# A two-layer graph network on one core: the output rows of layer 1 completed by accumulating DMAs

## The chip, the core and the metric

The kernel runs on one core of one Trainium2 chip. The time is device time in microseconds (us), and lower is better. The core has a matrix engine (TensorE, in the profile PE), an elementwise engine (VectorE, DVE), an activation engine (ScalarE, ACT), a general engine (GpSimd, POOL) and SyncE (SP), which here only issues DMAs. Each engine works through a queue of its own in order; they wait for each other by semaphores. SBUF is the on-chip memory; PSUM is the memory into which TensorE writes.

## What is computed

Two layers over N = 4096 nodes of 512 features, with a dense 4096 x 4096 matrix `adj`:

```python
h = relu(layernorm(x))
x = x + softmax(q @ k.T * scale + 2 * adj) @ v          # layer 0; q, k, v are projections of h
h = relu(layernorm(x))                                  # layer 1
nX = (h @ W) as 8 heads of 64, normalized per head, times a_ln, plus b_ln
kg = leaky_relu(at1 + at2.T) * adj                      # per head, at1 and at2 from nX
y = softmax(where(adj != 0, kg, -32768)) @ nX + nX      # "+ nX": the own features
x = x + elu(y)                                          # the residual
```

ELU is `y` where y is positive and `exp(y) - 1` elsewhere, so `elu(y) = relu(y) + (exp(-relu(-y)) - 1)`. The change is in how the last two lines are formed.

## The kernel before

The work has two stages. Layer 0 runs over 8 chunks of 512 target rows and 32 tiles of 128 source rows. It is led by TensorE. At the end of each chunk it writes the finished rows of layer 1's input to DRAM (`store_rows`, L457, into `x1_d`) and, spread over the next tiles, prepares layer 1: features, their statistics, and `own` (L358), which GpSimd computes and SyncE stores to `own_d`. `own` holds the own features with the constant that goes with them.

Layer 1 runs over 512 steps (`STEPS`, L897): 8 chunks of target rows, in each 2 groups of four heads (`hg`), in each 32 source tiles (`jt`). So a group of heads is 32 steps, and there are 16 groups. One step n does this:

- `z_sums` (L964), TensorE: the logits of four heads into two PSUM pairs `d`.
- `relu` (L987), ScalarE: relu of one pair into the SBUF tile `t`.
- `leaky` (L992), VectorE: for each of the other two heads a maximum and an addition (L999), then a multiplication by the adjacency tile `g` (L1004), of one head or, in a "light" step, of two; then the addition that ends the leaky relu of the first two heads (L1005).
- `weigh` (L1007), GpSimd: the multiplication by `g` of the remaining three heads, or of two in a light step (L1012). In the profile these are operations of 128x1536 and 128x1024.
- `exponent` (L1014), ScalarE, three steps later; `values` (L1017), TensorE, four steps later.

Which steps are light is a set of numbers (`light`, L904). The order is written by hand: every call under `seq` keeps its place in its engine's queue. DMAs without `seq` are placed by the scheduler.

When a group's last `values` is issued, `finish` (L1033) enters the group's remaining work into `later` under the following steps; `extra` then emits it at the middle or end of these. At step offsets 0 to 2 the sums are copied, turned into rows by TensorE and divided by their last column (`divide`, L1056), which also adds `own`. ELU follows with `minus`, `exps`, `positive` and `less_one` on ScalarE, `elu` (L1081) and `close` (L1085) on GpSimd, at offsets 4 to 10; `close` adds the residual `xi` and has SyncE store the result. `load_rows` (L956) loads `xi` and `own` for a group at its step 20: four DMAs of 256 KB, in pieces of 512 bytes.

Of the kernel before, what the change touches and what calls it, by code (L numbers as in the profile page):

```python
# [10 lines left out]
F32 = mybir.dt.float32  # L11
BF16 = mybir.dt.bfloat16
AF = mybir.ActivationFunctionType
ALU = mybir.AluOpType
# [4 lines left out]
P = 128  # L19
N = 4096  # L20
D = 512
NH = 8
HD = 64
NB = N // P
SB = 4
# [11 lines left out]
NI = N // GC  # L37
# [41 lines left out]
def fast_path(  # L79
# [18 lines left out]
    nc = tc.nc  # L98
    seq = tc.keep_in_program_order
# [14 lines left out]
    dram = ctx.enter_context(tc.tile_pool(name="dram", bufs=1, space=DRAM))  # L114
# [22 lines left out]
    s_d = dram.tile([NS, P, 4, KC // 2, 2, P], F32, name="s_d")  # L137
    q_d = dram.tile([NI, P, KC, GC], F32, name="q_d")
    t_d = dram.tile([NI, P, 4, KC // 2, GC // 2], F32, name="t_d")
    x1_d = dram.tile([N, D], F32, name="x1_d")  # L140

    gT_d = dram.tile([NB, P, N], F32, name="gT_d")
    nT_d = dram.tile([NB, P, N], BF16, name="nT_d")
# [4 lines left out]
    z1_d = dram.tile([P, 2, N], BF16, name="z1_d")  # L148

    nX_d = dram.tile([NB, P, D], F32, name="nX_d")  # L150

    own_d = dram.tile([N, D], F32, name="own_d")
    u4_d = dram.tile([NB, NH, P], F32, name="u4_d")
    at2_d = dram.tile([NB, P, NH], F32, name="at2_d")

    def inverse_root(engine, pool, v, n, name):

# [82 lines left out]
    def make_ready(ic, x1s, small, at_step, gap, last):  # L240

        n = SB * NH
# [3 lines left out]
        rows = slice(ic * SB, (ic + 1) * SB)  # L246
# [111 lines left out]
        def own(b):  # L358
            o = prep.tile([P, NH, HD], F32, name="own", tag="prod", bufs=2)
            seq(nc.gpsimd.tensor_mul(o, features(b), over_heads(aln_sb)))  # L360
            seq(nc.gpsimd.tensor_add(o, o, over_heads(bln2_sb)))
            nc.sync.dma_start(
                out=own_d[ts(ic * SB + b, P), :], in_=o.rearrange("p h e -> p (h e)")
            )

        def split():

# [59 lines left out]
        for b in range(SB):  # L427
            d = (0 if last else 2) + gap * b
# [27 lines left out]

    def store_rows(ic, x1s):  # L457
        for b in range(SB):
            seq(nc.sync.dma_start(out=x1_d[ts(ic * SB + b, P), :], in_=x1s[b]))


    with tc.tile_pool(name="early", bufs=2) as early, tc.tile_pool(name="kv", bufs=1) as kv:
        aa.extend(kv.tile([P, NH, HD], F32, name=f"a{e}_sb") for e in (1, 2))
        v = kv.tile([P, NB, D], F32, name="v")
# [68 lines left out]
        with tc.tile_pool(name="proj_c", bufs=1) as pc, tc.tile_pool(  # L533
            name="proj", bufs=2
# [137 lines left out]
            for sb in range(1, NS):  # L672
# [4 lines left out]
                if sb == 1:  # L677
                    seq(nc.sync.dma_start(
                        out=w1_sb.rearrange("p k h e -> p k (h e)"),
                        in_=w1.rearrange("(k p) o -> p k o", p=P),  # L680
# [16 lines left out]
        with tc.tile_pool(name="attn", bufs=2) as work, tc.tile_pool(  # L697
            name="attn_ps", bufs=2, space=PSUM
# [142 lines left out]
            for s in range(0, n_tiles, 2):  # L841
                ic, jt = TILES[s]
# [48 lines left out]
    with tc.tile_pool(name="ga_in", bufs=2) as inputs, tc.tile_pool(  # L891
# [8 lines left out]
        inverses = gat.tile([P, NI, 2, 2, 2, 4], F32, name="inverses")  # L900
        loads, logits, zs, groups = {}, {}, {}, {}


        light = {n for n in range(n_steps) if n % NB in (1, 8, 12, 13, 19, 25)}  # L904
        later = {}

        def load_adj(q):
# [40 lines left out]
        def pair_rows(ap, ic, hg):  # L948

            r, c = cols(ic, hg)  # L950
            return [
                ap[r, c.start + f * P : c.start + (f + 1) * P].rearrange("(b p) d -> p b d", p=P)
                for f in range(2)
            ]

        def load_rows(n):  # L956
            ic, hg, _ = STEPS[n]
            for name, src in (("xi", x1_d), ("own", own_d)):
                t = work.tile([P, 2, SB, 2 * HD], F32, name=name, tag=name, bufs=1)
                for f, ap in enumerate(pair_rows(src, ic, hg)):  # L960
                    nc.sync.dma_start(out=t[:, f], in_=ap)
                groups[ic, hg][name] = t

        def z_sums(n):  # L964

# [67 lines left out]
        def finish(n, ic, hg):  # L1033

            grp = groups.pop((ic, hg))
            ob = work.tile([P, 2, GC], F32, name="ob", tag="ob", bufs=1)
            y = grp["own"].rearrange("p f b (h e) -> p f (b h) e", e=HD)

            def room():
                grp["e"] = work.tile([P, 2, SB * 2, HD], F32, name="e", tag="ob", bufs=1)  # L1040

            def copies():
                for hf in range(2):
                    seq(nc.scalar.copy(ob[:, hf, :], grp["acc"][hf]))

            def to_rows(hf):
                pt = psum.tile([P, 2, GC], F32, name="pt1", tag="d", bufs=3)
                for b in range(SB):
                    col = (b % 2) * 2 * HB
                    seq(nc.tensor.matmul(  # L1050
                        pt[:, b // 2, col : col + 2 * HB], ob[:, hf, ts(b, P)],
                        back.rearrange("p e c -> p (e c)"), start=True, stop=True,
                    ))
                grp["pt"] = pt[:, :, 0 : 4 * HB].rearrange("p k (q c) -> p k q c", c=HB)

            def divide(hf):  # L1056
                v = grp.pop("pt")
                rinv = inverses[:, ic, hg, hf]
                seq(nc.vector.reciprocal(rinv, v[:, :, :, HD]))
                v = v[:, :, :, 0:HD]  # L1060
                seq(nc.vector.tensor_mul(v, v, rinv.unsqueeze(3).to_broadcast([P, 2, 4, HD])))
                own = y[:, hf].rearrange("p (k q) e -> p k q e", k=2)
                seq(nc.vector.tensor_add(own, v, own))

            def flat(t):
                return t.rearrange("p f q e -> p (f q e)")

            def minus(hf):
                seq(nc.scalar.activation(grp["e"][:, hf], y[:, hf], AF.Relu, scale=-1.0))

            def exps(hf):
                e = grp["e"][:, hf]
                seq(nc.scalar.activation(e, e, AF.Exp, scale=-1.0))

            def positive():
                seq(nc.scalar.activation(flat(y), flat(y), AF.Relu))

            def less_one():
                seq(nc.scalar.add(flat(grp["e"]), flat(grp["e"]), -1.0))

            def elu():  # L1081
                e = flat(grp["e"])
                seq(nc.gpsimd.tensor_add(e, e, flat(y)))  # L1083

            def close():  # L1085
                e = grp["e"]
                seq(nc.gpsimd.tensor_add(  # L1087
                    flat(e), flat(e), grp["xi"].rearrange("p f b d -> p (f b d)")
                ))
                for f, ap in enumerate(pair_rows(out, ic, hg)):  # L1090
                    nc.sync.dma_start(
                        out=ap, in_=e[:, f].rearrange("p (b h) e -> p b (h e)", h=2)
                    )

            for d, place, f in (
                (0, "mid", copies),
                (1, "mid", lambda: to_rows(0)), (1, "end", lambda: divide(0)),
                (2, "mid", lambda: to_rows(1)), (2, "end", lambda: divide(1)),
                (4, "end", room), (4, "end", lambda: minus(0)), (5, "end", lambda: minus(1)),
                (6, "end", lambda: exps(0)), (6, "end", positive), (7, "end", lambda: exps(1)),  # L1100
                (8, "end", less_one),
                (9, "end", elu), (10, "end", close),
            ):
                later.setdefault((n + d, place), []).append(f)

# [30 lines left out]
            for f in later.pop((n, place), []):  # L1136
                f()

        for n in range(n_steps + 15):

            q = n // JB + 1
            if n == 1:
# [1 line left out]
            if n % JB == (2 if q == NS - 1 else 0) and q < n_steps // JB:  # L1144
                load_adj(q)
                if q < NS:
                    load_features(q)
            if n < n_steps and STEPS[n][2] == 20:
                load_rows(n)
            if n + 10 < n_steps and STEPS[n + 10][2] == 0:  # L1150
                open_group(n + 10, nc.sync)
            extra(n, "top")
# [447 lines left out]
```

## Time and profile before

| what | value |
|---|---|
| median of 3 runs | 3955.43 us (3955.2 to 3957.88) |
| profiled execution | 3958.11 us |
| its span | 3956.2 us |
| TensorE busy | 3699.6 us, 94% |
| VectorE busy | 2915.4 us, 74% |
| GpSimd busy | 2501.9 us, 63% |
| ScalarE busy | 1779.3 us, 45% |
| mean TensorE clock granted | 0.99 |
| first VectorE operation of layer 1 (L999) | at 2092.05 us |

A share of the span is an average over two stages. In the page's row of 40 slices (a digit is the busy share in tenths) the two can be told apart:

```profile
PE   8989999999999999999997799999999999999997
...
DVE  5435556565565656556556799999999999999997
ACT  1001011111111111111114688888888888888887
POOL 3432225243342525234156899999999999999998
```

Layer 0 is the part in which only PE stands at 9. Layer 1 begins at about slice 22, and from there PE, VectorE and GpSimd are all at 9. In that second part the largest groups of instructions are, with count, busy time and mean duration of one, and then the idle time of the engine before them and what ended it (window from 2200 us to the end):

```profile
L1012 POOL TENSOR_TENSOR t<-t,g 128x1536 f32<-128x1536 f32 x401 | 1381.3, 3502 | 42.2 <-DVE t L1005 42.2
...
L1012 POOL TENSOR_TENSOR t<-t,g 128x1024 f32<-128x1024 f32 x92 | 220.7, 2399 | 18.6 <-DVE t L1005 13.5 <-DVE nX L1119 5.0
...
L1087 POOL TENSOR_TENSOR e<-e,xi 128x1024 f32<-128x1024 f32 x16 | 38.2, 2386 | 0.1
L1083 POOL TENSOR_TENSOR e<-e,own 128x1024 f32<-128x1024 f32 x16 | 38.0, 2376 | 12.3 <-ACT e L1079 12.3
...
L1061 DVE TENSOR_TENSOR pt<-pt,inverses 128x512 f32<-128x512 f32 x32 | 22.4, 700 | 1.1
L1063 DVE TENSOR_TENSOR own<-pt,own 128x512 f32<-128x512 f32 x32 | 22.1, 691 | 1.1
```

L1083 and L1087 are GpSimd's two additions at the end of a group, L1063 is VectorE's addition of `own`. The durations of neighbours overlap by some 0.05 us, so that sums of durations come out a little above the elapsed time.

### The profile page before, as it was taken

To read this page: it belongs to the slowest core of one execution; us is meant where nothing else is said; L and a number is where in the kernel's file an instruction comes from. 1 tells how busy PE (TensorE), PEld (TensorE's weight loads), DVE (VectorE), ACT (ScalarE), POOL (GpSimd) and SP (SyncE) were. 2 spreads that over 40 slices of the span, in tenths; PEclk is the share of its full clock that TensorE was granted. 3 is DMA by queue.
4 is the path that set the end of the run, shared out by engine and by line. 5 is a ranking of instruction groups with operands and counts; after the bars stand their busy time and mean duration, and the time that the engine had idled before them with its cause. 6 is when DMAs were issued, how large, how long until landed. Compare 5 with 4: busy or idle time off the path is not lost. (4 is left out here: it accounts for less than half of the span.)

```text
span 3956.2 us, 48595 instructions
## 1 busy us (share of the span) xinstructions
PE 3699.6 (94%) x17418; PEld 1720.8 (43%) x17418; DVE 2915.4 (74%) x4331; ACT 1779.3 (45%) x1581; POOL 2501.9 (63%) x1305
## 2 busy tenths in 40 slices
PE   8989999999999999999997799999999999999997
PEld 4446666666666666666662222222222222222222
DVE  5435556565565656556556799999999999999997
ACT  1001011111111111111114688888888888888887
POOL 3432225243342525234156899999999999999998
PEclk9999999999999999999998999999999999999999
DMA  6466666767675766758557766666666666665563
GB/s 205 178 201 193 204 183 199 206 187 218 177 228 158 217 192 183 222 174 230 151 174 190 191 186 187 184 186 175 169 180 181 184 181 184 180 185 172 172 181 111
DMA packets 624059, 737.79 MB, mean 186 GB/s; under 512 B 83904, under 2 KB 467136, under 8 KB 604352
## 3 DMA queue, kind: packets, MB, share of 16 engines
q1 hardware_dynamic: 621744, 732.83, 64.5%
q8 instruction: 138, 2.26, 0.2%
q10 hardware_dynamic: 2064, 1.77, 0.2%
q14 instruction: 113, 0.93, 0.1%
HBM read 562.23 MB, written 172.23 MB: 186 GB/s over the span
## 5 line engine op out<-in xcount | busy, mean ns | idle before, releaser
L1012 POOL TENSOR_TENSOR t<-t,g 128x1536 f32<-128x1536 f32 (+1 forms) x512 | 1655.3, 3293 | 98.3 <-DVE t L1005 66.4
L1028 PE MATMUL acc<-t,nX 128*64 128x512 f32 x4096 | 994.1, 606 | 41.0 <-ACT t L1015 35.9
L752 POOL TENSOR_TENSOR total<-total,aT 128x512 f32<-128x512 f32 x248 | 340.4, 1372 | 1060.1 <-ACT aT L747 1053.0
L1015 ACT ACTIVATE t<-t 128x2048 f32<-128x2048 f32 x512 | 974.9, 1904 | 2.0 <-POOL t L1012 2.0
L762 PE MATMUL acc<-v,aT 128*128 128x512 f32 x2048 | 961.7, 592 | 0.0
L747 ACT ACTIVATE aT<-aT 128x512 f32<-128x512 f32 x256 | 161.2, 630 | 1323.4 <-DVE aT L742 1315.4
L989 ACT ACTIVATE t<-d 128x1024 f32<-128x1024 f32 x512 | 524.8, 1025 | 319.4 <-PE d L981 319.2
L1005 DVE TENSOR_TENSOR t<-t,d 128x1024 f32<-128x1024 f32 x512 | 619.9, 1211 | 6.6 <-ACT t L989 6.6
L973 PE MATMUL d<-z,z 6*128 6x512 bf16 x2048 | 382.7, 387 | 140.5 <-DVE t L1004 76.5
L762 PEld LDWEIGHTS acc<-v,aT 128*128 128x128 f32 x2048 | 389.1, 190 | 273.1 <-issue 245.1
L1028 PEld LDWEIGHTS acc<-t,nX 128*64 128x64 f32 x4096 | 250.2, 136 | 552.1 <-issue 351.8
L999 DVE SCALAR_TENSOR_TENSOR d<-u,at2m,d 128x512 f32<-128x512 f32 x608 | 456.2, 750 | 33.3 <-PE d L981 29.8
L742 DVE TENSOR_TENSOR aT<-aT,X 128x256 f32<-128x256 f32 x512 | 214.8, 419 | 279.9 <-PE X L734 276.8
L1004 DVE TENSOR_TENSOR t<-d,g 128x512 f32<-128x512 f32 (+1 forms) x512 | 402.0, 785 | 16.6 <-DMA g<-gT_d 7.0
L973 PEld LDWEIGHTS <-z 6*128 6x128 bf16 x2048 | 94.4, 91 | 663.2 <-issue 400.9
L742 DVE TENSOR_TENSOR aT<-aT,Z 128x256 f32<-128x256 f32 x384 | 159.5, 415 | 291.3 <-PE Z L734 286.7
L999 DVE SCALAR_TENSOR_TENSOR t<-u,at2m,d 128x512 f32<-128x512 f32 x416 | 310.8, 747 | 43.2 <-DVE d L999 1.4
L981 PE MATMUL d<-nb,ident_b 64*64 64x512 bf16 x2048 | 319.9, 391 | 2.7 <-DMA nb<-nT_d 2.7
L981 PE MATMUL d<-nx,ident_b 64*64 64x512 bf16 x2048 | 320.3, 391 | 1.1 <-DMA nx<-nT_d 1.1
L726 DVE SCALAR_TENSOR_TENSOR gs<-ng,aT 128x512 f32<-128x512 bf16 x256 | 285.9, 1117 | 10.4 <-DMA gT_d<-gs 1.8
L734 PE MATMUL Z<-qt,hS 128*128 128x256 f32 x1024 | 265.9, 382 | 8.7 <-DVE aT L742 8.3
L734 PE MATMUL X<-qt,hS 128*128 128x256 f32 x1024 | 264.0, 380 | 0.0
(171 smaller groups left out, 3204.2 us busy)
## 6 DMA issues: line engine op xcount, KB each, us to landing
g<-gT_d SPq DMA_DIRECT2D x128, 1024.0 KB, 5.5
ag<-in_adj_dram SPq DMA_DIRECT2D x256, 256.0 KB, 5.7
hT<-h_d SPq DMA_DIRECT2D x64, 1024.0 KB, 5.9
hS<-s_d SPq DMA_DIRECT2D x64, 1024.0 KB, 8.2
gT_d<-gs SPq DMA_DIRECT2D x256, 256.0 KB, 3.0
nb<-nT_d SPq DMA_DIRECT2D x128, 512.0 KB, 4.5
nx<-nT_d SPq DMA_DIRECT2D x256, 256.0 KB, 5.4
nT_d<-ng SPq DMA_DIRECT2D x256, 128.0 KB, 3.4
```

Of the source, the lines that this page charges most:

```text
L734: seq(nc.tensor.matmul(out, a, b, start=start and k == 0, stop=k == 1, skip_group_check=not start,))
L742: seq(nc.vector.tensor_add(p, p, part))
L762: seq(nc.tensor.matmul(sums[ic][b], probs[s][:, ts(b, P)], v[:, jt, :], start=jt == 0, stop=jt == NB - 1))
L973: seq(nc.tensor.matmul(pair[hh // 2][:, hh % 2, :], z2[rows, ts(jt % JB, P)], groups[ic, hg]["z1"][rows, :], start=True, stop=False,))
L981: seq(nc.tensor.matmul(pair[hh // 2][ts(c, HD), hh % 2, :], ident_b[rows, rows], masks[r != c][rows, jt % JB, :], start=False, stop=True,))
L989: seq(nc.scalar.activation(t[:, 0:2, :], zs[n][0], AF.Relu, scale=4.0))
L999: seq(nc.vector.scalar_tensor_tensor(pair[1][:, e, :] if e > 1 - mine else t[:, 2, :], u4[:, e, :], at2m[:, jt, h : h + 1], pair[1][:, e, ...
L1004: seq(nc.vector.tensor_mul(t[:, HG - mine : HG, :], pair[1][:, 2 - mine : 2, :], g))
L1005: seq(nc.vector.tensor_add(t[:, 0:2, :], t[:, 0:2, :], pair[0]))
L1012: seq(nc.gpsimd.tensor_mul(t[:, 0:mine, :], t[:, 0:mine, :], g))
L1015: seq(nc.scalar.activation(logits[n], logits[n], AF.Exp))
L1028: seq(nc.tensor.matmul(grp["acc"][hf][ts(e, HD), :], nX[jt // SB][:, jt % SB, hg * HG + 2 * hf + e, :], t[:, 2 * hf + e, :], start=jt == 0 ...
```

## The change

Three elementwise additions of `finish` become accumulating DMAs, issued from GpSimd's queue (`add`):

- `divide` now only multiplies, out of PSUM into a new tile `y`. At step offset 3 a DMA adds the group's block of `own_d` to `y`.
- `elu` is replaced by a DMA that adds `y` to `e` in SBUF, at offset 11.
- The addition in `close` is replaced by a DMA that adds the block of `x1_d` to `e`, at offset 14. `close` keeps only the stores, at offset 17.

So that each of these transfers reads one contiguous run of 4 KB for each partition, `own_d` and `x1_d` are laid out by chunk and head group, and every block is stored by two DMAs (`store_block`) in place of one. `load_rows` and its tiles go. ScalarE's operations of ELU stand two offsets later. The set of light steps becomes four of 32 (11, 17, 23, 29) in place of six (1, 8, 12, 13, 19, 25): in a light step VectorE multiplies two heads and GpSimd two. The loop runs seven steps longer at its end, to have room for the later offsets.

```diff
-    x1_d = dram.tile([N, D], F32, name="x1_d")
+    x1_d = dram.tile([NI, 2, P, 2, SB, P], F32, name="x1_d")
...
-    own_d = dram.tile([N, D], F32, name="own_d")
+    own_d = dram.tile([NI, 2, P, 2, SB, P], F32, name="own_d")
...
+    def store_block(queue, ap, ic, b, rows):
+        for g in range(2):
+            seq(queue.dma_start(
+                out=ap[ic, g, :, :, b, :],
+                in_=rows[:, ts(g, 2 * P)].rearrange("p (f d) -> p f d", d=P),
+            ))
...
-            nc.sync.dma_start(
-                out=own_d[ts(ic * SB + b, P), :], in_=o.rearrange("p h e -> p (h e)")
-            )
+            store_block(nc.sync, own_d, ic, b, o.rearrange("p h e -> p (h e)"))
...
-            seq(nc.sync.dma_start(out=x1_d[ts(ic * SB + b, P), :], in_=x1s[b]))
+            store_block(nc.sync, x1_d, ic, b, x1s[b])
...
-        light = {n for n in range(n_steps) if n % NB in (1, 8, 12, 13, 19, 25)}
+        light = {n for n in range(n_steps) if n % NB in (11, 17, 23, 29)}
...
-        def load_rows(n):
-            ic, hg, _ = STEPS[n]
-            for name, src in (("xi", x1_d), ("own", own_d)):
-                t = work.tile([P, 2, SB, 2 * HD], F32, name=name, tag=name, bufs=1)
-                for f, ap in enumerate(pair_rows(src, ic, hg)):
-                    nc.sync.dma_start(out=t[:, f], in_=ap)
-                groups[ic, hg][name] = t
...
-            y = grp["own"].rearrange("p f b (h e) -> p f (b h) e", e=HD)
+            y = work.tile([P, 2, SB * 2, HD], F32, name="y", tag="y", bufs=1)
...
-                v = v[:, :, :, 0:HD]
-                seq(nc.vector.tensor_mul(v, v, rinv.unsqueeze(3).to_broadcast([P, 2, 4, HD])))
-                own = y[:, hf].rearrange("p (k q) e -> p k q e", k=2)
-                seq(nc.vector.tensor_add(own, v, own))
+                seq(nc.vector.tensor_mul(
+                    y[:, hf].rearrange("p (k q) e -> p k q e", k=2), v[:, :, :, 0:HD],
+                    rinv.unsqueeze(3).to_broadcast([P, 2, 4, HD]),
+                ))
+
+            def add(t, what):
+                seq(nc.gpsimd.dma_start(out=flat(t), in_=what, accum_op=ALU.add))
+
+            def of_group(ap):
+                return ap[ic, hg].rearrange("p f b d -> p (f b d)")
...
-            def elu():
-                e = flat(grp["e"])
-                seq(nc.gpsimd.tensor_add(e, e, flat(y)))
...
-                seq(nc.gpsimd.tensor_add(
-                    flat(e), flat(e), grp["xi"].rearrange("p f b d -> p (f b d)")
-                ))
...
-                (4, "end", room), (4, "end", lambda: minus(0)), (5, "end", lambda: minus(1)),
-                (6, "end", lambda: exps(0)), (6, "end", positive), (7, "end", lambda: exps(1)),
-                (8, "end", less_one),
-                (9, "end", elu), (10, "end", close),
+                (3, "end", lambda: add(y, of_group(own_d))),
+                (6, "end", room), (6, "end", lambda: minus(0)), (7, "end", lambda: minus(1)),
+                (8, "end", lambda: exps(0)), (8, "end", positive), (9, "end", lambda: exps(1)),
+                (10, "end", less_one), (11, "end", lambda: add(grp["e"], flat(y))),
+                (14, "end", lambda: add(grp["e"], of_group(x1_d))), (17, "end", close),
...
-        for n in range(n_steps + 15):
+        for n in range(n_steps + 22):
...
-            if n < n_steps and STEPS[n][2] == 20:
-                load_rows(n)
```

## The prediction

> **What bounds the kernel now.** I read the page's 40 slices first: TensorE carries the first half, and from slice 23 VectorE and GpSimd both stand at 9 tenths. The change lies in that second part (layer 1), so next came the busy time over one head group (32 steps), with columns for the stretch, its length, then busy time and instruction count of each engine, TensorE's clock and the DMA share:
>
> ```profile
> 3278.09:3389.86 111.77, 101.90 (x658) 28.09 (x657) 107.55 (x135) 94.73 (x72) 108.05 (x35) 1.00 0.63 180
> ```
>
> A group takes 111.77 us. VectorE (third figure, 107.55) and GpSimd (fifth, 108.05) are equally busy, so busy time doesn't say who leads. The waits between 2300 and 3900 us do:
>
> ```profile
> POOL t L1012 <- DVE t L1005: 47.2, 62, 1.4
> ...
> DVE d L999 <- PE d L981: 7.6, 14, 0.5
> ```
>
> GpSimd waited 47.2 us for VectorE; VectorE waited 0.5 us a group for TensorE and never for GpSimd. VectorE leads. Its timeline around a division, a plain step and a light one (start, duration) gives prices as start-to-start distances, which leave nothing out:
>
> ```profile
> 3160.09 1.21 DVE L1005 TENSOR_TENSOR t<-t,d 128x1024 f32<-128x1024 f32 x1
> 3161.32 0.21 DVE L1059 RECIPROCAL inverses<-pt 128x8 f32<-128x8 f32 x1
> 3161.57 0.70 DVE L1061 TENSOR_TENSOR pt<-pt,inverses 128x512 f32<-128x512 f32 x1
> 3162.30 0.69 DVE L1063 TENSOR_TENSOR own<-pt,own 128x512 f32<-128x512 f32 x1
> 3162.91 0.75 DVE L999 SCALAR_TENSOR_TENSOR d<-u,at2m,d 128x512 f32<-128x512 f32 x1
> ...
> 3170.97 0.75 DVE L999 SCALAR_TENSOR_TENSOR d<-u,at2m,d 128x512 f32<-128x512 f32 x1
> ...
> 3174.22 1.54 DVE L999 SCALAR_TENSOR_TENSOR d<-u,at2m,d 128x512 f32<-128x512 f32 x2
> ...
> 3178.12 0.75 DVE L999 SCALAR_TENSOR_TENSOR d<-u,at2m,d 128x512 f32<-128x512 f32 x1
> ```
>
> Plain step 3.25 us (3170.97 to 3174.22), light step 3.91, the two divisions 3.27 together. 26 x 3.25 + 6 x 3.91 + 3.27 + 0.5 = 111.7: the group is VectorE's sum. GpSimd's timeline over the same period (a row merges equal lines, whatever their shape; the first row holds 20 plain and 3 light steps):
>
> ```profile
> 3201.88 75.58 POOL L1012 TENSOR_TENSOR t<-t,g 128x1536 f32<-128x1536 f32 x23
> 3278.09 3.47 POOL L1012 TENSOR_TENSOR t<-t,g 128x1536 f32<-128x1536 f32 x1 [0.63 <-DVE t L1005]
> 3282.91 6.89 POOL L1012 TENSOR_TENSOR t<-t,g 128x1536 f32<-128x1536 f32 x2 [1.35 <-DVE t L1005]
> 3290.06 2.38 POOL L1012 TENSOR_TENSOR t<-t,g 128x1024 f32<-128x1024 f32 x1 [0.25 <-DVE t L1005]
> 3293.30 10.34 POOL L1012 TENSOR_TENSOR t<-t,g 128x1536 f32<-128x1536 f32 x3 [0.87 <-DVE t L1005]
> 3304.33 2.38 POOL L1012 TENSOR_TENSOR t<-t,g 128x1024 f32<-128x1024 f32 x1 [0.69 <-DVE t L1005]
> 3306.65 2.39 POOL L1083 TENSOR_TENSOR e<-e,own 128x1024 f32<-128x1024 f32 x1
> ```
>
> Light step 2.33 (3304.33 to 3306.65), plain step (75.58 - 3 x 2.33) / 20 = 3.43, and the idle brackets add up to 3.79. 26 x 3.43 + 6 x 2.33 + two additions of 2.33 = 107.8, plus 3.8 idle: the same 111.6. GpSimd's whole reserve is 3.8 us a group.
>
> Last, the start of layer 1: a wait of SyncE, then VectorE's first step there.
>
> ```profile
> SPq L961 <- DVE x L809: 22.2, 1, 22.2
> ```
>
> ```profile
> 2097.77 0.69 DVE L1004 TENSOR_TENSOR t<-d,g 128x512 f32<-128x512 f32 x1 [4.18 <-DMA g<-gT_d]
> ```
>
> The first load of `xi` waits for layer 0's last division, and the first `z2`, `nb`, `nx` and `g` stand behind it; the first step then waits for `g`.
>
> **What the Trainium skill says.** "DMA: Bandwidth & Descriptors", section "SWDGE vs HWDGE vs iDMA": a DMA that accumulates can only be issued from GpSimd, whose cores compute the descriptors in software. So the transfers cost time on the engine with 3.8 us of reserve. "Specifications" there gives about 1 us to the first byte on that path. The trace of before has no GpSimd DMA, so neither is seen in it. "Rules for kernel authors" there: an accumulate reads its destination and writes it later, so whoever touches those bytes must wait; in the changed order the third transfer does wait for the second. "SBUF — State Buffer", section "Who interferes with whom": a VectorE instruction with at most one SBUF input does not hinder GpSimd. Here each large VectorE operation has one operand in PSUM, and GpSimd's plain steps keep 3.43 us, which agrees.
>
> **The change part by part, for one group.**
>
> VectorE. Two light steps become plain: 2 x (3.91 - 3.25) = 1.32 saved. The two additions of `own` go: 2 x (0.61 start to start, plus 0.1 of the dependent gap) = 1.4. The multiplication writes SBUF in place of PSUM; L1004, which also reads PSUM and writes SBUF, takes 0.68 against its 0.70, so nothing. New sum: 28 x 3.25 + 4 x 3.91 + 1.87 + 0.5 = 109.0, or 2.7 less.
>
> GpSimd. 28 x 3.43 + 4 x 2.33 = 105.4; both additions go; three transfers come, each costing c. The changed program has 48 of them, 16 x 3, none split. c lies between 0.4 (the 0.37 that SyncE takes to issue `g`) and 3 (an estimate: the page "DMA: Bandwidth & Descriptors", section "Anatomy of one DMA", fits 2.0 us of fixed cost, mostly completion; if all of it stood on the engine and the second read added half). I take 1.0. Then GpSimd needs 108.4 and stays just below VectorE. They meet at c = (109.0 - 105.4) / 3 = 1.2, and at c = (111.8 - 105.4) / 3 = 2.1 the group is where it was.
>
> ScalarE. The same operations two steps later. New is that `minus` waits for the first transfer. Behind it stand the next exponential and the next relu, which VectorE's L1005 needs. Room: GpSimd ends a step's product about 3 us before VectorE begins the step three later; ScalarE reaches `minus` one step and a relu after that, 3 + 3.25 + 1 = 7 us after GpSimd starts the transfer, and roughly 1 us more before VectorE notices. A landing of c + 4.4 (what the 512 KB `nb` takes) + about 1 for the second read = 6.4 fits narrowly. Bound: from nothing to 2 us a group. The third transfer has three products, 3.43 + 3.43 + 2.33 = 9.2 us, until it waits for the second: nothing.
>
> Traffic. Per group 1 MB of loads in 512-byte pieces goes, three 512 KB accumulations come; at a DMA share of 0.63 that is nothing in itself. In layer 0 each stored block takes two issues on SyncE, 0.3 us each for 56 more; SyncE mostly waits for VectorE there: 0 to 4 us, taken as 0.
>
> Start of layer 1. Without `load_rows` the first `z2` waits only for layer 0's last score product (2071 us) and `g` for nothing new. They can be issued about 11 us earlier, and VectorE can start when its statistics end at 2085.5; L1004 at about 2087 in place of 2097.8. The 1 MB of step 20 also leaves a stretch with a DMA share of 0.90. Later waits on features and on GpSimd's preparation may eat some, and GpSimd has two fewer light steps there: 2 to 14 us, taken as 9.
>
> End. The last group loses two GpSimd additions (4.7) and 1.3 on VectorE, and gains three transfers in series of 1 + 3.3 us each (12.9): 7 us later, between 3 and 15.
>
> Sum over the 15 groups that end inside the layer: -15 x 2.7 - 9 + 7 = -43 against the profiled execution of 3958.1 us (span 3956.2). It stands 2.7 above the median of the runs, so I forecast 3955.4 - 43 = 3912.
>
> **The rivals.**
>
> 1. GpSimd becomes the bound: c between 1.2 and 2.1. At 1.6 a group takes 105.4 + 4.8 = 110.2, so -15 x 1.6 - 9 + 9 = -24: 3931. For it: the reserve is thin, and the accumulation has two reads to describe. Against: 1 us is the page's figure.
> 2. The transfer lands late, `minus` holds ScalarE and so VectorE: at 10 us in place of 8 that gives back 2 x 15 = 30: 3942. For it: DMA engines are busy 0.63 of the time. Against: the room of 7 to 8 us.
> 3. The slower side: writing the descriptors holds GpSimd for more than about 2.1 us. At c = 3 a group takes 114.4, 15 x 2.6 = +39, -9 at the start, +13 at the end: 3998. For it: nothing in the trace bounds c above. Against: the page's 1 us.
>
> **How the numbers follow.** Forecast 0.50 (own range 3900 to 3922), rival 1 0.23, rival 2 0.08, rival 3 0.19. The range runs from 3900 (start -14, the 0.5 us wait gone) to 3965, leaving out most of rival 3. A change of 0.2% (8 us) is about what a measurement here can tell. Faster: all of the forecast, most of rival 1 and half of rival 2, 0.74; same 0.07; slower 0.19.
>
> **What would show it.** Right: groups of about 109 us, GpSimd idle under 1.5 us a group and gaps of about 1 us at its transfers, no wait of ScalarE for them, the first L1004-kind operation of layer 1 before 2090 us, an end some 7 us longer. Wrong: VectorE waiting for GpSimd or ScalarE, gaps above 2 us on GpSimd, ScalarE's `minus` waiting for `own_d`.

## The result and the profile after

| | before | after |
|---|---|---|
| median | 3955.93 us (6 runs) | 3942.53 us (6 runs, 3940.43 to 3948.62) |
| ratio after/before | | 0.9967, 95% interval 0.9954 to 0.998 |
| span of the profiled execution | 3956.2 us | 3943.6 us |

The change gains 13 us, where 43 were forecast. To see where, I cut both traces at the same events: layer 0's last reciprocal, with which its last division begins, the first division of the first and of the last head group, and the end. These are the two profiled executions, which took 3958.1 and 3945.4 us.

| stretch | before | after | difference | forecast |
|---|---|---|---|---|
| up to layer 0's last reciprocal | 2079.2 | 2094.0 | +14.9 | 0 |
| from there to the first group's division | 187.3 | 174.7 | -12.6 | -9 |
| the 15 groups up to the last one's division | 1671.4 | 1645.0 | -26.4 | -41 |
| from there to the end | 18.4 | 29.9 | +11.5 | +7 |
| sum | 3956.2 | 3943.6 | -12.6 | -43 |

In the changed kernel's lines, L996 and L1002 are VectorE's L999 and L1005 of before, L1009 is GpSimd's product, L1057 the multiplication of `divide`, L1063 an accumulating transfer, L978 the score product of TensorE, L1072, L1076, L1079 and L1082 are ScalarE's `minus`, `exps`, `positive` and `less_one`, L1012 is the exponential, and L159 a store of `own` or `x1`.

**A steady group.** Busy time over one group (length of the stretch, then busy time and count of each engine, TensorE's clock, DMA share):

```profile
3264.25:3373.68 109.43, 101.22 (x660) 27.94 (x657) 105.02 (x133) 94.76 (x72) 108.15 (x36) 1.00 0.73 189
```

109.43 us in place of 111.77. GpSimd (fifth figure) is as busy as before: the transfers and two more plain steps fill what the additions left. The waits between 2300 and 3900 us:

```profile
DVE d L996 <- PE d L978: 15.6, 30, 2.1
DVE t L1001 <- DMA g<-gT_d: 6.0, 4, 2.5
...
POOL t L1009 <- DVE t L1002: 20.1, 39, 1.7
...
ACT e L1072 <- DMA y<-own_d: 1.0, 3, 0.4
```

GpSimd's wait for VectorE has more than halved (47.2 before). VectorE's for TensorE's `d` has doubled (7.6 before), and `g` has become late four times, all of them in the early groups, before 2860 us. ScalarE's `minus` (L1072) waited 1.0 us in all for the transfer. VectorE's timeline around a division and a light step:

```profile
3155.62 0.75 DVE L996 SCALAR_TENSOR_TENSOR d<-u,at2m,d 128x512 f32<-128x512 f32 x1
...
3159.10 0.69 DVE L1057 TENSOR_TENSOR y<-pt,inverses 128x512 f32<-128x512 f32 x1
3159.78 0.76 DVE L996 SCALAR_TENSOR_TENSOR d<-u,at2m,d 128x512 f32<-128x512 f32 x1
...
3176.02 1.54 DVE L996 SCALAR_TENSOR_TENSOR d<-u,at2m,d 128x512 f32<-128x512 f32 x2
...
3179.93 0.75 DVE L996 SCALAR_TENSOR_TENSOR d<-u,at2m,d 128x512 f32<-128x512 f32 x1
```

The step with a division takes 4.16 us (3155.62 to 3159.78), so a division costs 0.91 over a plain step; the light step is 3.91 as before. 28 x 3.25 + 4 x 3.91 + 1.82 = 108.5; of the other 1.0 us, 0.85 are two waits for `d` in each group (0.49 and 0.36). GpSimd's timeline around the three transfers:

```profile
3166.61 0.88 POOL L1063 DMA_DIRECT2D y<-own_d  x1
3167.23 26.66 POOL L1009 TENSOR_TENSOR t<-t,g 128x1536 f32<-128x1536 f32 x8
3193.83 0.89 POOL L1063 DMA_DIRECT2D e<-y  x1
3194.45 9.49 POOL L1009 TENSOR_TENSOR t<-t,g 128x1536 f32<-128x1536 f32 x3
3203.62 1.17 POOL L1063 DMA_DIRECT2D e<-x_d  x1
3204.52 19.78 POOL L1009 TENSOR_TENSOR t<-t,g 128x1536 f32<-128x1536 f32 x6
```

Start to start, the transfers cost GpSimd 0.62, 0.62 and 0.90 us. The page's rows from issue to landing:

```profile
y<-own_d POOLq DMA_DIRECT2D x16, 512.0 KB, 5.6
e<-y POOLq DMA_DIRECT2D x16, 512.0 KB, 5.1
e<-x_d POOLq DMA_DIRECT2D x16, 512.0 KB, 8.0
```

**Layer 0.** From the second on, every chunk is 1.4 to 3.9 us longer (228.3 in place of 226.5 as a rule), 15.3 us over the seven, and nearly all of that is lost at one place in each, ahead of tile 28. TensorE's wait there between 100 and 2110 us (1.1 us in all before):

```profile
PE Z L740 <- DMA hT<-h_d: 14.1, 7, 2.8
```

SyncE's queue at such a place, and TensorE's product that uses `hT`, before:

```profile
902.96 0.34 SPq L362 DMA_DIRECT2D own_d<-own  x1
903.39 0.38 SPq L530 DMA_DIRECT2D hT<-h_d  x1
...
908.42 1.13 PE L734 MATMUL Z<-qt,hT 128*128 128x256 f32 x4
```

and after:

```profile
903.98 1.84 SPq L159 DMA_DIRECT2D own_d<-own  x3
905.93 0.55 SPq L536 DMA_DIRECT2D hT<-h_d  x1
...
911.28 1.13 PE L740 MATMUL Z<-qt,hT 128*128 128x256 f32 x4 [1.57 <-DMA hT<-h_d]
```

Three stores stand right ahead of the load of `hT` where one stood; the load is issued 2.5 us later, on a timeline that itself runs 1.4 us later at this point, and TensorE, which leads this layer, waits for it.

**Start and end of layer 1.** SyncE's wait for layer 0's last division is gone; what is left of it is this one, and VectorE's first multiplication by `g` (L1001):

```profile
SPq L915 <- PE X L740: 10.4, 1, 10.4
```

```profile
2103.72 0.68 DVE L1001 TENSOR_TENSOR t<-d,g 128x512 f32<-128x512 f32 x1
```

The first `z2` now goes out behind layer 0's last score product, and the multiplication stands 9.7 us behind layer 0's last reciprocal, where it stood 18.6 us behind it (2097.77 us). The end, on GpSimd and ScalarE:

```profile
3915.84 0.89 POOL L1063 DMA_DIRECT2D y<-own_d  x1 [7.19 <-DVE y L1057]
...
3921.86 1.15 ACT L1072 ACTIVATE e<-y 128x512 f32<-128x512 f32 x2 [8.63 <-DMA y<-own_d]
...
3926.38 0.87 POOL L1063 DMA_DIRECT2D e<-y  x1 [9.64 <-ACT e L1082]
3931.50 0.87 POOL L1063 DMA_DIRECT2D e<-x_d  x1 [4.25 <-DMA e<-y]
3936.98 0.93 SPq L1087 DMA_DIRECT2D out_dram<-e  x2
```

From each transfer to what waited for it: 6.0, 5.1 and 5.5 us, one behind the other, with nothing to cover them.

### The profile page after: what moved, and what is told of

The parts are those of the page before. It is cut to its first block, busy times and chain, and to the rows that moved or that the text cites. A ratio compares the mean times of both kernels' runs of the same rounds, so it can differ in the third digit from the quotient of the medians.

```text
span 3943.6 us, 48614 instructions
## 1 busy us (share of the span) xinstructions
PE 3697.2 (94%) x17418; PEld 1722.2 (44%) x17418; DVE 2869.3 (73%) x4299; ACT 1779.9 (45%) x1581; POOL 2501.3 (63%) x1321
## 5 line engine op out<-in xcount | busy, mean ns | idle before, releaser
L1009 POOL TENSOR_TENSOR t<-t,g 128x1536 f32<-128x1536 f32 (+1 forms) x512 | 1704.8, 3531 | 55.7 <-DVE t L1002 48.1
L1012 ACT ACTIVATE t<-t 128x2048 f32<-128x2048 f32 x512 | 974.9, 1905 | 1.5 <-POOL t L1009 1.5
L1002 DVE TENSOR_TENSOR t<-t,d 128x1024 f32<-128x1024 f32 x512 | 619.2, 1209 | 2.8 <-ACT t L986 2.8
L970 PE MATMUL d<-z,z 6*128 6x512 bf16 x2048 | 370.9, 387 | 108.2 <-DVE t L1001 59.4
L996 DVE SCALAR_TENSOR_TENSOR d<-u,at2m,d 128x512 f32<-128x512 f32 x576 | 431.7, 749 | 39.2 <-PE d L978 34.9
L1001 DVE TENSOR_TENSOR t<-d,g 128x512 f32<-128x512 f32 (+1 forms) x512 | 383.9, 750 | 14.4 <-DMA g<-gT_d 7.8
L996 DVE SCALAR_TENSOR_TENSOR t<-u,at2m,d 128x512 f32<-128x512 f32 x448 | 334.5, 747 | 46.5 <-DVE d L996 1.4
L978 PE MATMUL d<-nx,ident_b 64*64 64x512 bf16 x2048 | 321.2, 392 | 1.4 <-DMA nx<-nT_d 1.2
L978 PE MATMUL d<-nb,ident_b 64*64 64x512 bf16 x2048 | 320.7, 392 | 0.0
L740 PE MATMUL X<-qt,hT 128*128 128x256 f32 x1024 | 264.3, 381 | 0.5 <-DVE aT L748 0.5
```

What stands on the lines that cost most here:

```text
L740: seq(nc.tensor.matmul(out, a, b, start=start and k == 0, stop=k == 1, skip_group_check=not start,))
L970: seq(nc.tensor.matmul(pair[hh // 2][:, hh % 2, :], z2[rows, ts(jt % JB, P)], groups[ic, hg]["z1"][rows, :], start=True, stop=False,))
L978: seq(nc.tensor.matmul(pair[hh // 2][ts(c, HD), hh % 2, :], ident_b[rows, rows], masks[r != c][rows, jt % JB, :], start=False, stop=True,))
L996: seq(nc.vector.scalar_tensor_tensor(pair[1][:, e, :] if e > 1 - mine else t[:, 2, :], u4[:, e, :], at2m[:, jt, h : h + 1], pair[1][:, e, ...
L1001: seq(nc.vector.tensor_mul(t[:, HG - mine : HG, :], pair[1][:, 2 - mine : 2, :], g))
L1002: seq(nc.vector.tensor_add(t[:, 0:2, :], t[:, 0:2, :], pair[0]))
```

## The experiments

Times are medians, each with its ratio to the kernel before, measured in the same series on the same chip (before: 3954.9 to 3955.9 us). "Stores moved" stands for the second row. An interval is 5 to 13 us wide; what two rows with overlapping intervals differ by is read from the traces.

| run | made from | us | ratio, 95% interval |
|---|---|---|---|
| one store a block | after | 3938.09 | 0.9955 (0.9938 to 0.9971) |
| own's stores behind the loads | after | 3926.31 | 0.9925 (0.9908 to 0.9942) |
| before, with the four light steps only | before | 3938.05 | 0.9958 (0.9942 to 0.9975) |
| after, with six light steps | after | 3953.34 | 0.9995 (0.9986 to 1.0003) |
| last group's additions on VectorE | stores moved | 3916.36 | 0.99 (0.9884 to 0.9917) |
| ELU spread over more steps | stores moved | 3936.88 | 0.9954 (0.9937 to 0.997) |
| no own for the last chunk | after | 3937.32 | 0.9956 (0.9939 to 0.9972) |
| six half transfers | stores moved | 3942.65 | 0.997 (0.9959 to 0.998) |
| one ELU operation a step | last group's additions on VectorE | 3908.93 | 0.9881 (0.9865 to 0.9898) |
| a fifth light step in four groups | one ELU operation a step | 3909.73 | 0.9882 (0.9865 to 0.9898) |
| store one step later | stores moved | 3926.49 | 0.9925 (0.9909 to 0.9942) |
| one load put back | stores moved | 3950.84 | 0.9987 (0.998 to 0.9994) |

### Layer 0: how many stores, and where

One store a block, from the changed kernel:

```diff
-    x1_d = dram.tile([NI, 2, P, 2, SB, P], F32, name="x1_d")
+    x1_d = dram.tile([NI, P, 2, 2, SB, P], F32, name="x1_d")
...
-    own_d = dram.tile([NI, 2, P, 2, SB, P], F32, name="own_d")
+    own_d = dram.tile([NI, P, 2, 2, SB, P], F32, name="own_d")
...
-        for g in range(2):
-            seq(queue.dma_start(
-                out=ap[ic, g, :, :, b, :],
-                in_=rows[:, ts(g, 2 * P)].rearrange("p (f d) -> p f d", d=P),
-            ))
+        seq(queue.dma_start(
+            out=ap[ic, :, :, :, b, :].rearrange("p g f d -> p (g f) d"),
+            in_=rows.rearrange("p (k d) -> p k d", d=P),
+        ))
...
-                return ap[ic, hg].rearrange("p f b d -> p (f b d)")
+                return ap[ic, :, hg].rearrange("p f b d -> p (f b d)")
```

> The changed kernel with own_d and x1_d laid out so that both head groups of a partition follow each other: each block is again stored by one DMA, in the same 512-byte pieces; the accumulating DMAs read the same 4 KB runs. Theory (issues): in layer 0 the changed kernel is 14.5 us longer because two more stores stand ahead of the load of hT in SyncE's queue, once in each chunk, so TensorE waits for hT before tile 28. Then layer 0 falls back to the chunk period of before, 226.5 us, and the time is some 14 us below the changed kernel, near 3928. Rival (pieces): the 512-byte pieces make the stores slow and these hold up the load; then layer 0 stays as long as in the changed kernel, and the time stays near 3942.

Neither came out in full. The first chunk ends between 496.3 and 500.4 us in the profiled runs, so I compare the seven chunks behind it. They take 1581.2 us before, 1596.5 after and 1586.7 here. Of the 15.3 us, 9.8 go with the doubled issues; 5.5 stay with as many issues as before, and most of that is again TensorE's wait for `hT`, 5.6 us in all. What then still differs from before at this place of the queue is the store's layout, pieces of 512 bytes in place of whole rows of 2 KB. That the layout makes these 5.5 us is left over, not tested by itself.

Both stores kept, but `own` one step later:

```diff
-                at_step(d + 12 + b // 2, own, b)
+                at_step(d + 13 + b // 2, own, b)
```

> The changed kernel with the own features of layer 0's chunks computed and stored one tile later, so that both stores of each block stand behind the load of hT and hS in SyncE's queue; number and pieces of the stores unchanged. Theory (issues ahead of the load): TensorE's wait before tile 28 goes, layer 0 is 13 to 15 us shorter, about 3928. Rival (the DMA engines are simply fuller, or stores of masks are held up so that VectorE waits): layer 0 stays within 3 us of the changed kernel, about 3942.

The time fell by 16.2 us, and the seven chunks take 1577.5 us, 3.6 below before. The queue in the same chunk:

```profile
894.16 1.36 SPq L536 DMA_DIRECT2D hT<-h_d  x1
...
902.36 1.20 SPq L159 DMA_DIRECT2D own_d<-own  x2
```

The load of `hT` goes out 8 us ahead of the stores, and TensorE no longer waits for it. (The computation of `own` on GpSimd moves along with its stores.) So all of layer 0's loss was the place of the stores ahead of this load; their number, and perhaps their layout, only set its size. In the kernel before the load stood behind two of these stores already, which fits that layer 0 is now shorter than there.

### The groups: which half of the change gives what

The four light steps alone, put into the kernel before:

```diff
-        light = {n for n in range(n_steps) if n % NB in (1, 8, 12, 13, 19, 25)}
+        light = {n for n in range(n_steps) if n % NB in (11, 17, 23, 29)}
```

> The kernel before with the four light steps of the change alone; additions, loads and stores as before. VectorE's sum falls by 1.3 to 110.4 us a group, GpSimd's rises to 28 x 3.43 + 4 x 2.33 + 4.7 = 110.0. Theory (VectorE leads by its sum, GpSimd has reserve): groups of 110.4 to 110.8, about -17 us, 3938. Rival (GpSimd needs its reserve at these places because its lag grows over thirteen plain steps in a row): groups stay near 111.8 and the time at 3955.

The reverse edit, the changed kernel with the six light steps of before:

> The changed kernel with the six light steps of before. VectorE's sum is 109.4 + 1.3 = 110.75 us a group, GpSimd's 26 x 3.43 + 6 x 2.33 + 2.1 for three transfers = 105.3. Theory: groups of 110.75 throughout, also in the groups in which GpSimd still prepares own features (110.8 there in the changed kernel), so about +1.3 x 9 = +12 us, 3954. Rival (the shift of work to GpSimd costs as much as it gives): the time stays at 3942 or falls.

| version | steady group, us | gain |
|---|---|---|
| before | 111.77 | |
| four light steps only | 110.10 | 1.67 |
| transfers only (after, with six light steps) | 109.83 | 1.94 |
| both (after) | 109.43 | 2.34 |

One line of numbers alone gives as much as the whole change (0.9958 and 0.9967, with intervals that overlap), and without it the change gives nothing that can be told (0.9995). With this line alone GpSimd leads: 28 x 3.43 + 4 x 2.33 + 2 x 2.33 = 110.0, and its wait for VectorE between 2300 and 3880 us falls from 47.2 to 3.1 us. So the transfers, which relieve GpSimd too, have something to add.

But the gains don't add up: alone they are 3.61 together, in the changed kernel 2.34. With six light steps VectorE never waits for `d` between 2300 and 3880 us, and its sum is the group: 26 x 3.25 + 6 x 3.91 + 1.82 = 109.8. With four the sum falls by 1.3, and waits of 0.85 take most of it back.

The time of the reverse edit is the expected one (3954), but its steady group isn't (109.83 for 110.75), so that agreement is partly chance. Over all 15 intervals between groups the traces have 1671.4 us before, 1656.5 with the light steps only, 1646.4 with the transfers only and 1645.0 with both: beside the transfers the light steps gained 1.4 us there, since the early groups grew (below). In the stretch ahead of these intervals, from layer 0's last reciprocal to the first group's division, they are worth 5 us with and without the transfers: 187.3 before, 182.3, 179.6 and 174.7. These are single traces, and this stretch takes from 174.7 to 179.0 us in five versions that don't differ in it.

ScalarE's timeline of the changed kernel shows what stands ahead of the longer of the two waits for `d`:

```profile
3290.36 0.62 ACT L1076 ACTIVATE e<-e 128x512 f32<-128x512 f32 x1
3290.88 1.05 ACT L1079 ACTIVATE y<-y 128x1024 f32<-128x1024 f32 x1
3291.82 1.90 ACT L1012 ACTIVATE t<-t 128x2048 f32<-128x2048 f32 x1
```

`exps` and `positive` run in one step and hold the exponential (L1012) back to 3291.82. TensorE's value product waited for that exponential and stands ahead of the next score product, and VectorE then waited for `d`:

```profile
3293.78 1.94 PE L1025 MATMUL acc<-t,nX 128*64 128x512 f32 x8 [1.21 <-ACT t L1012]
...
3296.43 0.76 DVE L996 SCALAR_TENSOR_TENSOR d<-u,at2m,d 128x512 f32<-128x512 f32 x1 [0.49 <-PE d L978]
```

First I spread ELU's operations over more steps, and with them moved the later transfers:

```diff
-                (8, "end", lambda: exps(0)), (8, "end", positive), (9, "end", lambda: exps(1)),
-                (10, "end", less_one), (11, "end", lambda: add(grp["e"], flat(y))),
-                (14, "end", lambda: add(grp["e"], of_group(x1_d))), (17, "end", close),
+                (8, "end", lambda: exps(0)), (9, "end", positive), (10, "end", lambda: exps(1)),
+                (11, "end", less_one), (12, "end", lambda: add(grp["e"], flat(y))),
+                (15, "end", lambda: add(grp["e"], of_group(x1_d))), (18, "end", close),
```

> The version with the stores of own behind the loads (3926.3), with the positive part moved to a step of its own: ScalarE then has one ELU operation a step at most, where two (0.62 and 1.05 us) stood ahead of one exponent. Theory (the two operations hold back the exponent, TensorE's value product stands behind that and the next score product behind both, so that VectorE waits 0.5 and 0.36 us for d in each group): these waits go, the steady group falls from 109.43 to about 108.6, the time to about 3914 us (3912 to 3919). Rival (GpSimd, which is idle only 1 us of 100 in a steady group, sets the lateness of the exponent): groups stay at 109.3 or more, the time within 3 us of 3926.

Neither: 10.6 us slower than the version that it was made from. The quiet groups did fall to 108.9, but nine of 14 intervals stood at 110.6 to 114.4, and VectorE's wait for `g` (2300 to 3900 us) says why:

```profile
DVE t L1001 <- DMA g<-gT_d: 17.3, 11, 2.2
```

The load of `g` was late 11 times, against twice in the version without this edit. Two things had moved along, the store and the two later transfers. The store alone, one step later:

```diff
-                (14, "end", lambda: add(grp["e"], of_group(x1_d))), (17, "end", close),
+                (14, "end", lambda: add(grp["e"], of_group(x1_d))), (18, "end", close),
```

> The version with own's stores behind the loads (3926.3), with the store of a group's rows one step later and nothing else moved: it then stands right ahead of the z1 and u4 loads of the next group and three steps ahead of a g load on SyncE's queue. Theory 1 (the longer groups of the version whose ELU was spread came from the place of this store on the queue): waits for g appear in five or more groups, groups of 110.5 to 112, the time 3933 to 3938 us. Theory 2 (they came from the accumulating transfers, one step later too and right ahead of a block of loads): no such waits, 3923 to 3930 us.

3926.5, as without the edit: not the store. That leaves the transfers; in the spread version the middle one was issued 0.2 to 0.3 us ahead of the 1 MB load of `g` in 15 of the 16 groups (4.4 us or more ahead of it without the edit). It landed after 9.4 us (median) in place of 5.1, and these loads of `g` took 6.4 to 8.2 us in place of 5.3 to 5.7. I didn't move the transfers alone, so this is left over by elimination and by these numbers. Then the waits for `d` again, with transfers and store in place (and with the end mended, below):

```diff
-                (6, "end", room), (6, "end", lambda: minus(0)), (7, "end", lambda: minus(1)),
-                (8, "end", lambda: exps(0)), (8, "end", positive), (9, "end", lambda: exps(1)),
-                (10, "end", less_one),
+                (6, "end", room), (6, "end", minus), (7, "end", positive),
+                (8, "end", exps), (9, "end", less_one),
```

> The version with own's stores behind the loads and the last group's additions on VectorE (3916.4), with ScalarE's ELU as one operation of all 1024 columns in each of four steps in a row (minus, positive, exps, less_one; 1.05 us or so each) in place of six operations in five steps, two of them in one step; transfers and store stay where they are. Theory (two ELU operations in one step, 1.67 us, hold back the exponent and through TensorE's order the next d): VectorE's waits for d fall from 0.85 us a steady group to 0.3 or less, the steady group from 109.45 to 108.6 to 108.9, the time to about 3908 us (3905 to 3912). Rival (GpSimd's lateness makes these waits): group and time as they were, 3914 to 3919.

The time is the expected one, 7.4 us less, and the steady group 109.03 (expected up to 108.9). VectorE's wait between 2830 and 3830 us, in the version without the edit and with it:

```profile
DVE d L996 <- PE d L978: 11.1, 19, 2.1
```

```profile
DVE d L996 <- PE d L978: 3.2, 10, 0.3
```

So it was ScalarE's two operations in one step. The edit also makes four operations out of six, but in the spread version, which keeps six and only takes the two apart, the quiet groups fell to 108.9 as well.

### The early groups, and what a transfer costs

After's first five intervals between groups are 112.72, 111.04, 110.58, 110.64 and 110.93 us, not 109.43. The third of them (columns as above):

```profile
2492.49:2603.07 110.58, 101.29 (x658) 27.92 (x656) 105.12 (x132) 94.84 (x73) 110.45 (x38) 1.00 0.72 189
```

GpSimd is busy 110.45 of 110.58 us, with two instructions more than in a steady group: here it is the bound. In the second and fourth it is idle 0.6 and 0.2 us. The changed kernel without the two GpSimd operations for `own` of the last chunk:

```diff
+            if ic == NI - 1:
+                return store_block(nc.sync, own_d, ic, b, x1s[b])
             o = prep.tile([P, NH, HD], F32, name="own", tag="prod", bufs=2)
```

> The changed kernel with GpSimd's two operations for own of the last chunk left out (the standardized features themselves are stored in their place, so that part of the product with aln and the addition of bln2 is missing for the last 512 rows). Theory (the second to fifth group are 110.6 to 111.0 because GpSimd, near its bound with the transfers, also makes own of the last chunk, 2 x 1.28 us a group): these four groups fall to 109.4 to 109.8, together 4 to 6 us, and the time to about 3937.5 us (3935 to 3941). Rival (the loads of the features and the stores at the start of layer 1 make these groups long): no change in them, 3942.

5.2 us less by the medians, 4.3 by the ratios, whose intervals overlap. The five intervals are 109.81, 109.46, 109.46, 110.92 and 109.46, together 6.8 less. GpSimd's reserve in a steady group is 1.3 us (109.43 - 108.15); these two operations (1.27 and 1.28 us) are more than that. The size is rough: in the version with `own`'s stores behind the loads the five intervals sum to 3.9 us less than after's, with no edit in them. The four light steps put into the kernel before show it too: two of its early groups took 112.4 and 114.4.

A fifth light step (n % 32 == 5) in the second to fifth group gives GpSimd that room, at VectorE's cost; made on the version with one ELU operation a step:

> The version with one ELU operation a step, with a fifth light step in each of the second to fifth group, where GpSimd also makes own of the last chunk. Theory (GpSimd runs up to 3.6 to 4.5 us late in these groups, and the load of g, which needs the tile that GpSimd read last, is late with it): VectorE takes 0.66 us more in each of the four groups and loses its waits there; the four groups, 444.4 us together in the version before this one's, fall to 437 to 440, and the time is 3 to 6 us below that of one ELU operation a step. Rival (the long early groups come from other transfers): the four groups gain nothing or grow by 2.6 us together.

In the trace GpSimd is at most 2.3 us late in these groups (4.1 without), and the four intervals sum to 440.15 us in place of 441.98. The median didn't move (3909.73 against 3908.93): below what this measurement can tell.

Is a transfer's cost on GpSimd one for each instruction, or does it go with the bytes?

```diff
-                seq(nc.gpsimd.dma_start(out=flat(t), in_=what, accum_op=ALU.add))
+                for f in range(2):
+                    seq(nc.gpsimd.dma_start(
+                        out=flat(t)[:, ts(f, GC)], in_=what[:, ts(f, GC)], accum_op=ALU.add,
+                    ))
```

> The version with the stores of own behind the loads (3926.3), with each accumulating transfer split in two halves of 512 columns: six issues a group, the same bytes. Theory 1 (GpSimd's time for a transfer is per instruction, 0.6 to 0.9 us each): GpSimd gets 2 us more a group and becomes the bound, groups about 110.4, the time about 3941 us (3936 to 3947). Theory 2 (the time goes with the descriptors or bytes, half for half a transfer): GpSimd's sum and the groups are unchanged at 109.4, 3926 us (3923 to 3931), and each issue takes about half as long.

```profile
3410.50 3.47 POOL L1064 DMA_DIRECT2D e<-y  x2
3411.67 11.57 POOL L1009 TENSOR_TENSOR t<-t,g 128x1536 f32<-128x1536 f32 x3
```

Two half transfers take 1.17 us start to start, 0.58 each (0.62 for a whole one), and the other two pairs of this group take 1.17 and 1.16: the cost is one for each instruction. The third whole transfer's 0.90 depends on where it falls, for in the spread version and with six light steps its median is 0.62; why stays open. Six of them are 3.5 us a group in place of 2.1, GpSimd's wait for VectorE falls from 17.5 to 4.4 us (2300 to 3860 us), and the time rises by 16.3. The way was another than expected, though: quiet groups stay at 109.44, and the loss comes in single groups of up to 114.8, with waits for `d` (20.1 us) and for `g` (12.7).

### The end and the start of layer 1

The last group's additions on VectorE, on the version with `own`'s stores behind the loads:

```diff
             def add(t, what):
+                if n == n_steps + 3:
+                    return seq(nc.vector.tensor_add(flat(t), flat(t), what))
...
+            if n == n_steps - 12:
+                last_own = load_last(own_d)
```

> The version with the last chunk's and every chunk's own stores behind the loads (3926.3), with one edit more: in the last group alone, whose end nothing covers, VectorE makes the three additions, from rows of own and x1 that plain loads bring in ahead. Theory (the end is longer because the three accumulating transfers stand one behind the other: issue to landing some 5.5, 5 and 6 us, 16.5 in all, against three additions of 1.2 us each): the end from the last reciprocal falls from 30 to about 17 us and the time to about 3914 us (3911 to 3916), the groups unchanged at 109.43. Rival (the end is ScalarE's ELU chain and the output's store): less than 4 us, 3922 or more.

The end fell from 30.1 to 17.5 us, the time by 10. After the last ELU operation two additions of 1.22 us are left:

```profile
3905.85 1.22 DVE L1072 TENSOR_TENSOR e<-e,y 128x1024 f32<-128x1024 f32 x1 [2.54 <-ACT e L1094]
3907.11 1.23 DVE L1072 TENSOR_TENSOR e<-e,rows 128x1024 f32<-128x1024 f32 x1
```

One load put back at step 20 of each group, on the same version (512 KB of `x1` into a tile `xi`; in the trace it is L964):

```diff
+            if n < n_steps and STEPS[n][2] == 20:
+                load_rows(n) 
```

> The version with the stores of own behind the loads (3926.3), with one load put back: at step 20 of each group a 512 KB load of the group's rows of x1 into a tile that nobody reads. On SyncE's queue the first of them stands again ahead of layer 1's first z2, nb, nx and g. Theory (the start of layer 1 gained because no such load stands there any more, waiting for layer 0's last division): the first step of layer 1 comes 8 to 12 us later, the groups stay at 109.4 us, the time is 3934 to 3939 us. Rival (the start gained from traffic or from the fewer light steps): under 3 us at the start, 3926 to 3930 us.

```profile
SPq L964 <- DMA xi<-x_d: 45.8, 9, 10.3
SPq L964 <- DVE x L815: 22.0, 1, 22.0
```

The wait of 22 us for layer 0's last division is back (second line), and the first `z2` goes out at 2081.4 in place of 2068.7. The first multiplication by `g` stands 18.0 us behind layer 0's last reciprocal in place of 10.6 (18.6 in the kernel before, 9.7 after the change). That is 7.4 us, a little under the 8 to 12 expected, and it shows that the late start was this load's place on the queue. The first group ends 12.8 us later, but the rest of that isn't clean: all 16 loads went out between 2081.0 and 2331.8 us, five of them before the first group's division, presumably as nobody reads the tile. They held the queue too (first line), the second group took 122.96 us in place of 109.84, and the total rose by 24.5 us, 12 to 17 more than expected. That part is the experiment's own and says nothing of the change.

## Why the prediction was wrong

The direction held, the size didn't: -13 for -43. Most of what is missing lies in two terms.

- **Layer 0, "0 to 4 us, taken as 0": +14.9.** This is the largest failed step. It priced 56 issues by their number and took SyncE's idle time as cover. But a queue works in order: what counted was which load stands behind the stores, and who waits for it. TensorE waited 14.1 us for that load in place of 1.1. Moved behind it, the same stores cost nothing.
- **"-15 x 2.7" for the groups: -26.4 in place of -41.** VectorE's own sum was right: 108.5 without waits. Two things were missed. The wait for `d` was carried over at 0.5 us and became 0.85, since ELU's two operations in one step hold the next exponential back: over 15 groups about 5 us. And GpSimd's reserve was weighed in a late group only; in the second to fifth group it also makes `own` of the last chunk, and is the bound in three of these four. After's first five intervals stand 8.8 us above five steady ones, before's don't; leaving these operations out takes 4 to 7 us of it.
- **c, taken as 1.0: 0.62 to 0.90.** GpSimd didn't become the bound of a steady group, and rivals 1 and 3 fell. The Trainium skill, "DMA: Bandwidth & Descriptors", section "SWDGE vs HWDGE vs iDMA", led rightly: the cost is on GpSimd. Its figure of about 1 us, in "Specifications" there, is a latency, not the engine's time; the trace has 0.6 to 0.9 for that.
- **`minus` waits "nothing": right**, 1.0 us in all. The first transfer lands after 5.6 us (6.4 estimated). Rival 2 fell, although its 3942 us is the time that came out: the number agrees by chance, the mechanism wasn't there.
- **Start, -9: -12.6.** Mechanism right: the first multiplication by `g` came 8.9 us earlier, counted from layer 0's last reciprocal, and with a load put back 7.4 us later. In time it came at 2103.7 us, behind the 2090 named, since layer 0 ended later. The rest of the gain lies in the first group and fits the 5 us that its two fewer light steps are worth; the prediction had named them only as something that could eat up part of the gain.
- **End, +7: +11.5.** Mechanism right, a transfer undersized: 4.3 us each was taken, 5.1 to 6.0 were measured.

## What to carry to other kernels

A DMA that is added to a queue can cost what stands behind it: look for the next load on that queue and the engine that waits for it, and place the store behind that load. When two engines are within 1% of each other, removing work from the leader shows the next wait, here a second operation in one step of ScalarE (busy 94.8 of 109.4 us), so gains that were measured alone don't add. Weigh the reserve of an engine in the early groups too, not only in a late one. A transfer in place of an addition pays where other work covers its 5 to 8 us; where nothing does, at the end, keep the addition. With the stores moved, ELU's operations taken apart, the last group's additions kept, and the changed kernel's transfers, the time is 3908.9 us, 1.2% below before. How much of that is the transfers' own isn't shown: no run has the four light steps and these mends without them.

## What was not expected of the hardware

An accumulating transfer of 512 KB holds GpSimd 0.62 to 0.90 us and one of 256 KB 0.58 us, so halving it buys nothing. From DRAM or from SBUF it lands after 5.1 to 8.1 us (medians); issued 0.2 to 0.3 us ahead of the 1 MB load of `g` it landed after 9.4 us, and that load took about 1 us longer.
